# A smooth convolution of images 1 to 3 as 36 products of 256 columns instead of 24 of 512

## The chip, the cores and the metric

The kernel runs on one core of a Trainium2 chip. The core has five engines with an instruction queue each, worked through in order: TensorE (PE, matrix products into the eight PSUM banks), VectorE (DVE), ScalarE (ACT), GpSimd (POOL) and SyncE (SP), whose queue here only starts transfers. Queues wait for one another through semaphores. The metric is the device time of one execution, in microseconds.

## The reference, cut to what matters

Four images of 256 channels and 64 x 64 pixels go through four layers, each of which adds its result to its normalised input. Only the first layer's convolution is concerned here:

```python
xs = conv(group_norm(x), smooth_w, 3x3, SAME) + smooth_b
xs = relu(group_norm(xs, gn1_w, gn1_b))
theta, phi, g = conv1x1(xs) three times
attn = softmax(theta^T phi)                # 4096 x 4096 for each image
y = attn g;  x = x + 0.1 * group_norm(conv1x1(y)) + xs
```

Layer 1 is a linear attention, layer 2 a depthwise 3x3 convolution with generated taps and a generated pointwise product, layer 3 a mixture of four 1x1 convolutions. All is fp32.

## The kernel before, in words

**Stages.** Image 0 is convolved alone (`convolve_first`). Then, for each image b, `project` makes theta, phi and g in `tpg`, and `attend(b)` computes the softmax attention in 128 steps. A step makes four PE products: two `pf` (logits, L655), which ACT turns into exponentials `pr` (L656), and two `py` (L694); DVE adds `pr` to the running total `tot` (L118). After 16 steps a chunk of 512 columns ends (`ended`): `inv` on DVE (L663) closes the total, PE sums it over partitions (`pss`, L667), DVE takes the reciprocal (L669) and makes `yt`, PE makes `ps_wy` (L678). Each of these is one step behind the one before.

**Weaving.** Other work is woven between the steps of the attention. In round 0 that is `scale_weights` and the convolution of image 1; in rounds 1 and 2 the layers 1 to 3 of the image before (`tail`) and then the convolution of the next image; in round 3 a tail alone. The last tail has nothing beside it. A `Chain` sets the pace: woven code yields numbers, and `yield n` lets `n * rate` attention steps pass. `w.later(k, f)` runs f after k further steps. So the source order fixes every queue, and a larger rate spreads the woven work over more steps. The rates are 1.5, 0.86, 0.86 and 1.24. Woven work that is not through when a round's 128 steps are over goes on alone.

**Convolution by products.** It is in a Winograd form. Over rows it makes four output rows from six (`TY`, `MY` = 6, 4): `down(a)` forms six row combinations of the input on DVE, in `ra` and `rt`. Over columns it makes two output columns from four (`TX`, `MX` = 4, 2): `across(k)` forms the tile `v` by one DVE operation of 1024 elements. `products(a, k)` multiplies v by the transformed filter, for two output and two input halves of the channels, 512 columns each (L403); `joined` adds the PSUM banks into the output row a, and `joining(a)` combines the rows a into the four rows of the image. For image 0, `filter_down` and `filter_across` form the filters on DVE, and `filter_across` writes all of them to DRAM (`filters`); images 1 to 3 read them back, 128 KB at a time.

**Depthwise taps.** In `tail`, `taps` runs 64 operations of a row part each on DVE (`yield 0.62` after each), eight for each of eight parts; after every second part `pointwise` follows on PE one and two steps later (`ps_pw`, L979), and `pointwise_added` on DVE.

**Buffers.** `k4` is a pool of ten tiles of 1024 elements (pr, tot, v, dw and others), `k2` of six of 512, `u` of four filter tiles.

Of the kernel before, what the change touches and what calls it, by code (L numbers as in the profile page):

```python
# [8 lines left out]
F32 = mybir.dt.float32  # L9
# [25 lines left out]
TY, MY, TX, MX = 6, 4, 4, 2  # L35
IY, IX = HW // MY, HW // MX

# [53 lines left out]
def conv_preact_fast(ctx: ExitStack, tc: tile.TileContext, guard, x, wc, wtpg, ww, wqkv, wout, w1cat, wd2,  # L91
# [11 lines left out]
    def k4(name):  # L103
        return wk.tile([P, CH], F32, tag="k4", name=name, bufs=10)
# [3 lines left out]
    def k2(name):  # L108
        return wk.tile([P, 512], F32, tag="k2", name=name, bufs=6)
# [20 lines left out]
    ra = cp.tile([P, NH, IY, HW + 2], F32, name="ra")  # L130
# [105 lines left out]
    filters = tc.dram_tile([TY, NH, P, TX, NH, P], F32, name="filters")  # L236
# [30 lines left out]
    def filter_across(a, stay=False):  # L267

        ends = u1[:, a].rearrange("p h (j o) -> p h j o", j=3)
        s, mid = (t.rearrange("p (h o) -> p h o", h=NH)  # L270
                  for t in (wk.tile([P, 512], F32, tag="inv", name="ends2"), k2("middle") if a == 4 else junk()))
        if stay:
            both = [k2("both_u").rearrange("p (h o) -> p h o", h=NH) for _ in range(2)]
        else:
            t = k4("both_u").rearrange("p (b h o) -> p b h o", b=2, h=NH)
            both = [t[:, b] for b in range(2)]
        nc.scalar.mul(mid, ends[:, :, 1], 0.5)
        tt(s, ends[:, :, 0], ends[:, :, 2], ALU.add)
        stt(both[0], s, 0.5, mid, ALU.mult, ALU.add)
        stt(both[1], s, 0.5, mid, ALU.mult, ALU.subtract)  # L280

        def of(k):
            return both[k - 1] if k in (1, 2) else ends[:, :, 0 if k == 0 else 2]

        for oh in range(NH):
            for k in range(TX):
                nc.sync.dma_start(out=filters[a, oh, :, k], in_=of(k)[:, :, bass.ts(oh, P)])
        return lambda k, oh, h: of(k)[:, h, bass.ts(oh, P)]

# [84 lines left out]
    def across(k, rows):  # L374

        def col(j):
            return rows[:, :, :, j:j + MX * (IX - 1) + 1:MX]

        v = k4("v")
        first, second, op = ((0, 2, ALU.subtract), (1, 2, ALU.add), (2, 1, ALU.subtract), (1, 3, ALU.subtract))[k]  # L380
        tt(v.rearrange("p (h y x) -> p h y x", h=NH, x=IX), col(first), col(second), op)
        return v

    ACROSS = (1, 2, 0, 3)

    def joiner(st):

        dst, one = [None] * NH, [None] * NH
# [9 lines left out]
        def products(a, k, v, u):  # L398

            ps = [bank("ps_conv") for _ in range(NH)]  # L400
            for oh in range(NH):
                for h in range(NH):
                    nc.tensor.matmul(ps[oh], u(oh, h), v[:, bass.ts(h, 512)], start=(h == 0), stop=(h == NH - 1))  # L403
                if k == 1:
                    one[oh] = k2("one").rearrange("p (y x) -> p y x", x=IX)
                    nc.scalar.copy(one[oh], ps[oh].rearrange("p (y x) -> p y x", x=IX))
            return ps

        def joined(a, k, ps):

            for oh in range(NH):
                p = ps[oh].rearrange("p (y x) -> p y x", x=IX)
                if k == 2:
                    take(a, oh)
                even, odd = dst[oh][:, :, 0::2], dst[oh][:, :, 1::2]
                if k == 2:
                    tt(even, one[oh], p, ALU.add)
                    tt(odd, one[oh], p, ALU.subtract)
                elif k == 0:
                    tt(even, even, p, ALU.add)  # L420
                else:
                    tt(odd, odd, p, ALU.subtract)
            return list(dst)
# [19 lines left out]
        def joining(a, oh, t):  # L443

            y0, y1, y2, y3 = (image[:, oh, :, j, :] for j in range(MY))
            if a == 2:
                return [(tt, y2, y1, t, ALU.add), (tt, y1, y1, t, ALU.subtract), (tt, y0, y0, y2, ALU.add)]
            if a == 4:
                both = k4("both").rearrange("p (y x) -> p y x", x=HW)
                return [(tt, both, y3, t, ALU.add), (tt, y3, y3, t, ALU.subtract), (tt, y0, y0, both, ALU.add),  # L450
                        (stt, y2, both, 4.0, y2, ALU.mult, ALU.add), (stt, y1, y3, 2.0, y1, ALU.mult, ALU.add),
                        (stt, y3, y3, 6.0, y1, ALU.mult, ALU.add)]
            return [(tt, y3, y3, t, ALU.add)] if a == 5 else []
# [5 lines left out]
        return products, joined, row_products, rows_joined, joining, stats  # L459
# [36 lines left out]
    def convolve(w, b):  # L496
# [4 lines left out]
        products, joined, _, rows_joined, joining, stats = joiner(st)  # L501
        PRODUCTS = [(a, k) for a in range(TY) for k in ACROSS]

# [7 lines left out]
        def multiply(a, k, v, u):  # L511
            ps = products(a, k, v, u)
            if k != 1:
                w.later(1, lambda: join(a, k, ps))

        def join(a, k, ps):
            dst = joined(a, k, ps)
            if k == 3 and a == 4:
# [7 lines left out]
            elif k == 3 and a == 2:  # L526
# [4 lines left out]
            elif k == 3:  # L531
# [4 lines left out]
        def load_filters(i):  # L536
            res = []
            for oh in range(NH):
                u = wk.tile([P, NH, P], F32, tag="u", name="u", bufs=4)
                nc.sync.dma_start(out=u, in_=filters[PRODUCTS[i][0], oh, :, PRODUCTS[i][1]])  # L540
                res.append(u)
            return lambda oh, h: res[oh][:, h, :]
# [3 lines left out]
        for i, (a, k) in enumerate(PRODUCTS):  # L546
            if k == 1:
                for op, *args in down(a, ra, ra):
                    op(*args)
                    yield 0.35  # L550
            v, u = across(k, ra), us
            if i + 1 < len(PRODUCTS):
                us = load_filters(i + 1)
            w.later(1, lambda a=a, k=k, v=v, u=u: multiply(a, k, v, u))
            yield 0.8
# [4 lines left out]
    def convolve_first(w):  # L560
# [5 lines left out]
        def across_all(a, rows):  # L566
            return [(a, k, across(k, rows), lambda oh, h, k=k: u[a](k, oh, h)) for k in ACROSS]
# [5 lines left out]
        products, joined, row_products, rows_joined, _, stats = joiner(st)  # L573
# [5 lines left out]
        u = {a: filter_across(a, stay=True) for a in (4, 3)}  # L579
# [13 lines left out]
        for i, (a, k, v, f) in enumerate(four):  # L593
            if i + 1 < TX:
                joined(*three[i + 1])
            filter_across((0, 1, 2, 5)[i])
# [3 lines left out]
        for i in range(1, TX):  # L600
# [149 lines left out]
    def linear_attention(w, b, big, qT, k4, st, sh, alone):  # L750
# [25 lines left out]
        def qkv(xg, s2, rinv):  # L776
# [4 lines left out]
            for j in range(4):  # L781
# [8 lines left out]
                yield 0.125  # L790
# [22 lines left out]
        for c in range(NC):  # L813
            if c + 1 < NC:
                ahead = normed(c + 1)
            yield 0.5
# [244 lines left out]
    def mixed(w, b, big, k4, st, sh, held):  # L1061
# [39 lines left out]
        for h in range(NH):  # L1101
            wm.append(mix[:, h, :] if held is None else wk.tile([P, NH * P], F32, tag="u", name="wmh", bufs=4))
# [51 lines left out]

    def run(*steps):
# [16 lines left out]
    with tc.manual_schedule(engines={E.PE, E.Activation, E.DVE, E.Pool, E.SP}):  # L1172
        run(Chain(convolve_first).steps())
        run(project())
        for b in range(B - 1):
            attention = attend(b)
            parts = [tail(b - 1, big, qT)] if b > 0 else [scale_weights]
            if b == 0:
                load_x(1)
            run(Chain(both(*parts, lambda w: convolve(w, b + 1)), 1.5 if b == 0 else 0.86).steps(), attention)  # L1180
# [8 lines left out]
        run(Chain(tail(B - 2, big, qT, held=held), 1.24).steps(), attention)  # L1189
# [596 lines left out]
```

## Time and profile before

| what | us |
|---|---|
| median of 3 runs (lowest, highest) | 3144.46 (3142.55, 3146.85) |
| profiled execution (its span) | 3145.76 (3144.0) |
| PE, DVE, ACT busy in the span | 3033.0, 2079.6, 1129.2 |
| image 0 | 0 to 146 |
| round 0: image 1 beside attention of image 0 | 190.8 to 738 |
| round 1: tail of 0 and image 2 | 782 to 1479 |
| round 2: tail of 1 and image 3 | 1523 to 2219.9 |
| round 3: tail of 2 | 2263 to 2836 |
| end: tail of 3 alone | 2836 to 3144 |

Between these lie the four projects of some 44 us each. In the profile a product of two matrices counts as two PE instructions. A line of the groups names line, engine, operation, output and inputs with their sizes; then count, busy time, mean length in ns, and the idle time of the engine before such instructions with what ended it. In a line of busy times by stage stand its start and end, its length, the busy time and count of each engine, the granted PE clock, the share of the DMA engines and GB/s. In a line of the order of time stand start, length, engine and what ran.

### The profile page before, as it was taken

What the parts mean: (1) busy time and instruction counts of PE and PEld (TensorE: products, weight loads), DVE (VectorE), ACT (ScalarE), POOL (GpSimd) and SP (SyncE); (2) the same over time, 40 slices, a digit from 0 to 9 for tenths busy, and PEclk for the clock granted to TensorE, in tenths of its full rate; (3) what the DMA queues carried; (4) which work ended last, traced back from release to release, by engine and by line L of the source; (5) the groups of instructions that cost most, each with busy time, mean ns of one, the idle gap of its engine ahead of it and who ended that gap; (6) DMA issues with size and microseconds to landing.
All of it is one profiled execution on the core that took longest, in us unless ns stands there. A gap on an engine that the chain in (4) does not pass through costs nothing.

```text
span 3144.0 us, 24213 instructions
## 1 busy us (share of the span) xinstructions
PE 3033.0 (96%) x8526; PEld 1472.9 (47%) x8526; DVE 2079.6 (66%) x2611; ACT 1129.2 (36%) x2097; POOL 131.6 (4%) x175
## 2 busy tenths in 40 slices
PE   6899999999999999999999999999999999996888
PEld 3454444445564444444565444444545544443533
DVE  8736766443547995877536896778363768855485
ACT  2233224332555332323364432222445443333510
POOL 0000000000010000000011000000100100000100
PEclk9999999999999999999999999999999999998999
DMA  5610013001100023113300102310410010120011
GB/s 184 182 34 26 32 35 66 7 14 47 67 11 21 20 74 116 39 39 67 114 8 3 41 20 77 110 44 31 113 62 1 11 34 14 47 74 34 14 60 65
DMA packets 73985, 161.68 MB, mean 51 GB/s; under 512 B 7936, under 2 KB 39424, under 8 KB 70912
## 3 DMA queue, kind: packets, MB, share of 16 engines
q1 hardware_dynamic: 69248, 143.27, 13.3%
q0 software_dynamic: 4608, 16.78, 2.9%
q8 instruction: 70, 1.15, 0.2%
q14 instruction: 59, 0.48, 0.0%
HBM read 103.40 MB, written 73.40 MB: 56 GB/s over the span
## 4 chain that ended last, share of the span: by engine, by line
PE 80%; DVE 12%; issue 5%; ACT 2%; DMA 0%; POOL 0%; SPq 0%; POOLq 0%; ACTq 0%
PE pf L655 23%; PE py L694 23%; PE ps_conv L403 8%; PE ps_qkv L784 5%; DVE dw L121 4%; PE ps_tp L631 4%; PE ps_ex L1117 3%; PE ps_pw L979 3%; DVE tot L118 2%; PE ps_g L636 2%; PE ps_wy L678 2%; PE ps_o L852 1%; PE ps_ctx L806 1%; PE ps_dw L1014 1%; PE ps_ss L770 1%
## 5 line engine op out<-in xcount | busy, mean ns | idle before, releaser
L656 ACT ACTIVATE pr<-pf 128x512 f32<-128x512 f32 x1024 | 604.2, 596 | 1227.3 <-PE pf L655 1214.2
L655 PE MATMUL pf<-tpg 128*128 128x512 f32 x2048 | 967.2, 595 | 1.4 <-ACT pr L656 1.4
L694 PE MATMUL py<-pr,tpg 128*128 128x512 f32 x2048 | 962.1, 592 | 3.0 <-ACT pr L656 2.9
L118 DVE TENSOR_TENSOR tot<-tot,pr 128x1024 f32<-128x1024 f32 x448 | 546.3, 1219 | 249.7 <-ACT pr L656 248.1
L694 PEld LDWEIGHTS py<-pr,tpg 128*128 128x128 f32 x2048 | 388.8, 190 | 494.3 <-issue 479.8
L655 PEld LDWEIGHTS pf<-tpg 128*128 128x128 f32 x2048 | 381.5, 190 | 443.0 <-issue 419.1
L121 DVE SCALAR_TENSOR_TENSOR dw<-xp,dk,dw 128x1008 f32<-128x1008 f32 x216 | 272.9, 1267 | 6.8 <-ACT dw L971 3.7
L403 PE MATMUL ps_conv<-v,u 128*128 128x512 f32 x576 | 259.0, 596 | 3.6 <-DVE v L118 3.6
L403 PEld LDWEIGHTS ps_conv<-v,u 128*128 128x128 f32 x576 | 109.7, 191 | 143.5 <-issue 136.6
L784 PE MATMUL ps_qkv<-wqkv_s,xg 128*128 128x384 f32 x384 | 129.9, 487 | 0.0
L631 PE MATMUL ps_tp<-big,wtpg_s 128*128 128x512 f32 x256 | 118.0, 605 | 3.0 <-ACT big L492 3.0
L118 DVE TENSOR_TENSOR tpg<-ps_g,bg_s 128x512 f32<-128x512 f32 x32 | 22.1, 691 | 145.6 <-PE ps_g L636 145.6
L210 POOL TENSOR_TENSOR rstd<-rstd,half 128x2 f32<-128x2 f32 x24 | 16.8, 700 | 2419.3 <-DVE rstd L315 2225.7
L979 PE MATMUL ps_pw<-dw,pk 128*128 128x512 f32 x224 | 104.6, 601 | 8.1 <-DVE dw L121 8.1
L669 DVE RECIPROCAL inv<-pss 128x512 f32<-128x512 f32 x32 | 107.3, 3352 | 7.2 <-PE pss L667 7.2
L784 PEld LDWEIGHTS ps_qkv<-wqkv_s,xg 128*128 128x128 f32 x384 | 72.2, 190 | 53.6 <-issue 9.6
L794 DVE TENSOR_REDUCE qs<-qk 128x16 f32<-128x512 f32 x24 | 16.5, 686 | 119.0 <-ACT qk L788 119.0
L118 DVE TENSOR_TENSOR v<-ra 128x1024 f32<-128x1024 f32 x72 | 86.7, 1219 | 0.4
L632 ACT ACTIVATE tpg<-ps_tp,btp_s 128x512 f32<-128x512 f32 x64 | 43.9, 687 | 119.6 <-PE ps_tp L631 119.6
L631 PEld LDWEIGHTS ps_tp<-big,wtpg_s 128*128 128x128 f32 x256 | 47.9, 195 | 55.0 <-issue 50.6
L854 ACT ACTIVATE junk<-ps_o 128x256 f32<-128x256 f32 x128 | 49.2, 384 | 67.5 <-PE ps_o L852 59.4
L979 PEld LDWEIGHTS ps_pw<-dw,pk 128*128 128x128 f32 x224 | 43.0, 192 | 62.6 <-issue 51.9
(281 smaller groups left out, 2904.6 us busy)
## 6 DMA issues: line engine op xcount, KB each, us to landing
u<-filters SPq DMA_DIRECT2D x144, 128.0 KB, 2.3
xp<-in_x_dram SPq DMA_DIRECT2D x16, 1024.0 KB, 6.3
xs_d<-big POOLq DMA_DIRECT2D x32, 512.0 KB, 11.7
wy_d<-wt SPq DMA_DIRECT2D x32, 512.0 KB, 3.0
out_dram<-res SPq DMA_DIRECT2D x64, 256.0 KB, 2.0
wy<-wy_d SPq DMA_DIRECT2D x28, 512.0 KB, 5.2
xs<-xs_d SPq DMA_DIRECT2D x24, 512.0 KB, 5.3
wp<-in_wp_dram SPq DMA_DIRECT2D x16, 512.0 KB, 4.6
```

Source lines behind the costliest of these rows:

```text
L118: nc.vector.tensor_tensor(o, a, b, op)
L121: nc.vector.scalar_tensor_tensor(o, a, s, b, op0, op1)
L403: nc.tensor.matmul(ps[oh], u(oh, h), v[:, bass.ts(h, 512)], start=(h == 0), stop=(h == NH - 1))
L631: nc.tensor.matmul(ps, wtpg_s[:, h, k, :], big[:, h, cols], start=(h == 0), stop=(h == NH - 1))
L636: nc.tensor.matmul(ps[:, j, :], big[:, h, bass.ts(4 * c + j, P)], wtpg_s[:, h, 2, :], start=(h == 0), stop=(h == NH - 1))
L655: nc.tensor.matmul(pf, phi[:, bass.ts(2 * m + s, P)], theta[:, bass.ts(q, 512)], start=True, stop=True)
L656: nc.scalar.activation(pr[:, bass.ts(s, 512)], pf, AF.Exp)
L669: nc.vector.reciprocal(inv, pss)
L694: nc.tensor.matmul(py, g[:, bass.ts(2 * m + s, P)], probs[i][:, bass.ts(s, 512)], start=(m == 0 and s == 0), stop=(m == NM - 1 and s == 1))
L784: nc.tensor.matmul(ps[:, 0:3 * HID], xg[:, h, bass.ts(j, P)], wqkv_s[:, h, :], start=(h == 0), stop=(h == NH - 1))
L979: nc.tensor.matmul(ps, pk[:, h * NH * P + oh * P:h * NH * P + (oh + 1) * P], dw[h][:, bass.ts(s, 512)], start=(h == 0), stop=(h == NH - 1))
L1117: nc.tensor.matmul(ps, wm[h][:, bass.ts(oh, P)], big[:, h, cols], start=(h == 0), stop=(h == NH - 1))
```

## The change

For images 1 to 3 the column form becomes the one that the rows have: four output columns from six (`TX`, `MX` = 6, 4). There are then 36 products of 256 columns (6 rows x 6 columns), each again for two output and two input halves. Image 0 keeps the old form, under new names (`across_first`, `products_first`, `joined_first`, `ACROSS1`).

- `across(pair)` forms two columns k of v together, (1, 2), (3, 4) or (0, 5), by three or four DVE operations; its inputs are columns of `ra` at a step of four elements. `products` puts both output halves of one k in one PSUM bank. `joined` first makes the sum and difference of a pair in `sums` (ACT one part, DVE two), and after pair (3, 4) writes four output columns by four operations at a step of four elements (`put`); pair (0, 5) is added by two more. Rows 4 and 5 are collected in `rt` instead of k4 tiles.
- `filter_across` serves rows 4 and 3 of image 0 alone, and writes nothing. `keep` stores the six rows of `filter_down` in DRAM (`rows_d`, 768 KB each). `filters_across`, a new part of round 0 behind `scale_weights`, loads each row into `big`, makes the four inner columns by six DVE operations of 512 elements, and stores them (`filters`, 1 MB a row). The outer columns are read from `rows_d` itself. A filter load is now 256 KB.
- `k4` has nine buffers instead of ten, `k2` five instead of six; `u` keeps four, of twice the size.
- Rates: 1.36 in round 0; 0.66 for the tail and 0.79 for the convolution in rounds 1 and 2; 1.28 in round 3. In `linear_attention` two yields shrink, 0.125 to 0.08 and 0.5 to 0.25.

```diff
-TY, MY, TX, MX = 6, 4, 4, 2
+TY, MY, TX, MX = 6, 4, 6, 4
...
-        return wk.tile([P, CH], F32, tag="k4", name=name, bufs=10)
+        return wk.tile([P, CH], F32, tag="k4", name=name, bufs=9)
...
-        return wk.tile([P, 512], F32, tag="k2", name=name, bufs=6)
+        return wk.tile([P, 512], F32, tag="k2", name=name, bufs=5)
...
+    def keep(rows):
+        for a in rows:
+            nc.sync.dma_start(out=rows_d[a], in_=u1[:, a].rearrange("p h (j o) -> p h j o", j=3))
...
-        for oh in range(NH):
-            for k in range(TX):
-                nc.sync.dma_start(out=filters[a, oh, :, k], in_=of(k)[:, :, bass.ts(oh, P)])
...
+    def filters_across(w):
+        n = NH * 3 * NH * P
+        for a in range(TY):
+            t = big[:, a % 2, 0:n].rearrange("p (h j o) -> p h j o", h=NH, j=3)
+            f = big[:, a % 2, n:n + (TX - 2) * NH * NH * P].rearrange("p (k h o) -> p k h o", k=TX - 2, h=NH)
+            nc.sync.dma_start(out=t, in_=rows_d[a])
+            first, mid, last = (t[:, :, j, :] for j in range(3))
+            for op, *args in ((tt, f[:, 0], first, last, ALU.add), (tt, f[:, 1], f[:, 0], mid, ALU.subtract),
+                              (tt, f[:, 0], f[:, 0], mid, ALU.add), (stt, f[:, 2], last, 4.0, first, ALU.mult, ALU.add),
+                              (stt, f[:, 3], mid, -2.0, f[:, 2], ALU.mult, ALU.add),
+                              (stt, f[:, 2], mid, 2.0, f[:, 2], ALU.mult, ALU.add)):
+                op(*args)
+                yield 0.3
+            nc.sync.dma_start(out=filters[a], in_=f)
...
+    def across(pair):
+        v = k4("v").rearrange("p (k n) -> p k n", k=2)
+        def cols(j):
+            return ra.rearrange("p h y x -> p (h y) x")[:, :, j:j + HW].rearrange("p r (i k) -> p k r i", k=MX)[:, 0:2]
+        vt = v.rearrange("p k (r i) -> p k r i", i=IX)
+        one, two = v[:, 0], v[:, 1]
+        def each(j, f, other):
+            return [(stt, vt[:, i], cols(j)[:, i], f, other[:, i], mul, add) for i in range(2)]
+        ops = {0: lambda: each(2, -5.0, cols(4)) + each(0, 4.0, vt),
+               1: lambda: each(1, -4.0, cols(3)) + [(tt, one, one, two, add), (stt, two, two, 2.0, one, mul, sub)],
+               3: lambda: [(tt, vt, cols(3), cols(1), sub), (stt, one, one, 2.0, two, mul, add),
+                           (stt, two, two, 2.0, one, mul, sub)]}
+        return v, ops[pair[0]]()
...
+        def products(pair, v, u):
+            banks = []
+            for i in range(2):
+                ps = bank("ps_conv")
+                for oh in range(NH):
+                    for h in range(NH):
+                        nc.tensor.matmul(ps[:, bass.ts(oh, IY * IX)], u[i][:, h, bass.ts(oh, P)],
+                                         v[:, i, bass.ts(h, IY * IX)], start=(h == 0), stop=(h == NH - 1))
+                banks.append(ps)
+            if pair != (0, 5):
+                parts[pair] = k4("sums").rearrange("p (k n) -> p k n", k=2)
+                nc.scalar.mul(parts[pair][:, 0], banks[0], -1 / 6 if pair == (1, 2) else 1 / 24)
+            return banks
...
+                    o = to[:, :, j::MX]
+                    stt(o, t, f, o if other is None else other, ALU.mult, ALU.add)
+            if pair == (0, 5):
+                put((0, 0.25, ps[0], None), (3, 1.0, ps[1], None))
+            elif not end:
+                stt(s[:, 1], ps[1], -f, s[:, 0], ALU.mult, ALU.add)
+                stt(s[:, 0], ps[1], f, s[:, 0], ALU.mult, ALU.add)
+            else:
+                near, far = parts[1, 2], parts[3, 4]
+                put(*((j, f, far[:, j % 2], near[:, j % 2]) for j, f in enumerate((1.0, 2.0, 4.0, 8.0))))
...
-            v, u = across(k, ra), us
+            (v, ops), u = across(pair), us
             if i + 1 < len(PRODUCTS):
                 us = load_filters(i + 1)
-            w.later(1, lambda a=a, k=k, v=v, u=u: multiply(a, k, v, u))
-            yield 0.8
+            for op, *args in ops:
+                op(*args)
+                yield 0.4
+            w.later(1, lambda a=a, pair=pair, v=v, u=u: multiply(a, pair, v, u))
+            yield 1
...
-                yield 0.125
+                yield 0.08
...
-            yield 0.5
+            yield 0.25
...
-            parts = [tail(b - 1, big, qT)] if b > 0 else [scale_weights]
+            parts = [at(0.66, tail(b - 1, big, qT))] if b > 0 else [at(1.36, both(scale_weights, filters_across))]
...
-            run(Chain(both(*parts, lambda w: convolve(w, b + 1)), 1.5 if b == 0 else 0.86).steps(), attention)
+            parts.append(at(1.36 if b == 0 else 0.79, lambda w: convolve(w, b + 1)))
+            run(Chain(both(*parts)).steps(), attention)
...
-        run(Chain(tail(B - 2, big, qT, held=held), 1.24).steps(), attention)
+        run(Chain(tail(B - 2, big, qT, held=held), 1.28).steps(), attention)
```

## The prediction

> **What bounds the kernel now.** I read the page's busy line and its chain first, then busy time by stage, then the order of time on PE and DVE inside a stage.
>
> ```profile
> PE 3033.0 (96%) x8526; PEld 1472.9 (47%) x8526; DVE 2079.6 (66%) x2611; ACT 1129.2 (36%) x2097; POOL 131.6 (4%) x175
> ...
> PE 80%; DVE 12%; issue 5%; ACT 2%; DMA 0%; POOL 0%; SPq 0%; POOLq 0%; ACTq 0%
> ...
> L403 PE MATMUL ps_conv<-v,u 128*128 128x512 f32 x576 | 259.0, 596 | 3.6 <-DVE v L118 3.6
> ```
>
> PE carries the chain, and the products to be changed are 259 us of it. By stage (image 0; project; rounds 0 to 3 with the projects between them; the end):
>
> ```profile
> core 0: us, PE busy (x) PEld busy (x) DVE busy (x) ACT busy (x) POOL busy (x), PEclk, DMA share, GB/s
> 0.00:146.00 146.00, 113.89 (x264) 50.82 (x264) 123.77 (x166) 26.90 (x39) 3.42 (x21) 0.98 0.54 186
> ...
> 190.80:738.00 547.20, 543.65 (x1272) 240.82 (x1271) 323.98 (x344) 185.35 (x310) 8.36 (x10) 1.00 0.10 26
> ...
> 782.00:1479.00 697.00, 689.49 (x1897) 329.62 (x1897) 515.77 (x646) 264.39 (x493) 33.08 (x39) 1.00 0.15 48
> ...
> 1523.00:2219.90 696.90, 689.40 (x1895) 329.40 (x1895) 515.89 (x647) 264.39 (x493) 33.10 (x39) 1.00 0.15 48
> ...
> 2263.00:2836.00 573.00, 573.00 (x1630) 279.77 (x1630) 371.47 (x456) 244.17 (x469) 27.18 (x29) 1.00 0.10 35
> ```
>
> In rounds 0 to 2, where the change works, PE idles 3.6 + 7.5 + 7.5 us. So a microsecond taken from PE is gained only while DVE keeps pace. Round 1 cut into 20.5 us pieces shows how near that is:
>
> ```profile
> 1069.00:1089.50 20.50, 20.50 (x49) 9.11 (x48) 20.29 (x21) 8.17 (x14) 0.00 (x0) 1.00 0.00 0
> 1089.50:1110.00 20.50, 20.50 (x49) 9.12 (x48) 20.22 (x21) 5.71 (x10) 0.00 (x0) 1.00 0.00 0
> ...
> 1438.00:1458.50 20.50, 19.18 (x47) 8.45 (x46) 20.33 (x31) 5.97 (x10) 0.00 (x0) 1.00 0.00 0
> ```
>
> The first two lie in the depthwise taps of the tail: both engines are full. The third is the end of the convolution: DVE is full and PE has begun to lose (1.3 us). The order of time gives the prices:
>
> ```profile
> 930.80 1.89 PE L852 MATMUL ps_o<-w,xp 128*128 128x256 f32 x8
> 932.53 1.88 PE L655 MATMUL pf<-tpg 128*128 128x512 f32 x4
> 934.25 1.88 PE L694 MATMUL py<-pr,tpg 128*128 128x512 f32 x4
> ```
>
> ```profile
> 1088.24 1.22 DVE L118 TENSOR_TENSOR tot<-tot,pr 128x1024 f32<-128x1024 f32 x1
> 1089.38 2.58 DVE L121 SCALAR_TENSOR_TENSOR dw<-xp,dk,dw 128x1024 f32<-128x1024 f32 x2
> 1091.88 1.22 DVE L118 TENSOR_TENSOR tot<-tot,pr 128x1024 f32<-128x1024 f32 x1
> ```
>
> Eight 256-column instructions start 1.73 us before the next group, so 0.216 us each; four of 512 take 1.72 us, 0.43 each (each product is two instructions). Half the columns cost half, weight load included. One attention step is 3.43 us of PE. On DVE, one tot and two taps take 3.64 us; back to back, an instruction starts some 0.04 us before its predecessor's recorded end.
>
> [...] the trace's 512-element rows have 683 to 692, so cutting an operation in two costs an extra 0.16 us. [...] The new column operations step by four fp32[...]. The trace has stride two at full speed (v<-ra, 1219 ns, like the contiguous tot) and no stride four. [...] 128 KB land in 2.3 us, 512 KB in 4.6 to 5.2, 1024 KB in 6.3.
>
> **The change, part by part.**
>
> *Products.* Per image 96 x 2 instructions of 512 (192 x 0.43 = 82.4 us) become 144 x 2 of 256 (288 x 0.216 = 62.3). Saved: 20 us an image, **60 us** in rounds 0 to 2, if PE does not wait instead.
>
> *DVE work of a convolution.* Removed per image: 24 x 1.22 (v) + 48 x 0.683 (joins out of PSUM) = 62 us. Added: 6 x 1.22 + 60 x 0.69 (v) + 60 x 0.69 (sums and results) = 90 us. The row-joining operations keep their number, and ACT swaps 12 copies for 12 scalings (0.59 each). So +28 us of DVE an image against -20 of PE. Mean load hides that; what stretches cannot hide follows.
>
> *Rates, rounds 1 and 2.* The order of DVE's instructions against the attention steps shows the tail ending near step 62 instead of 86, and products at steps 75 to 120 instead of 96 to 117. A tap (0.62 of a yield) now takes 0.62 x 0.66 = 0.41 steps, before 0.53. Taps stretch now: 64 taps and 8 pk sums fill 28 steps. PE: 28 x 3.43 + 64 x 0.43 (pointwise) + two chunk ends of 2.6 = 129 us. DVE: 64 x 1.265 + 8 x 0.75 + 16 x 1.37 (pointwise joins and statistics) + 26 tots x 1.22 + two chunk ends x 6.1 (reciprocal 3.35 and the rest) = 153, less 156 x 0.04 = 147. The excess is 18 us. Before, with 36.5 steps, PE had 158 and DVE 157: the full-but-free picture above. Each pointwise product stands one step behind its last tap and PE is in order, so behind a late tap wait pointwise, then pf and py. Lag is not carried over: **18 us** of waiting a round.
>
> The convolution keeps its mean: now 49 steps with PE 239 and DVE 219, before 24 steps with 168 and 154, 92% each. But the lumps grow. The row-4 joining beside a chunk end and the next rows has 65 us of DVE in ten steps with 51 of PE; the row-2 joining with a chunk end 24 in three steps with 11. In the old kernel such excesses of up to about 6 us passed with 1.3 us lost. I take 14 - 6 and 13 - 6, **15 us**, less the 2.5 lost now.
> Rounds 1 and 2 together: 2 x (-20 + 18 + 15 - 2.5) = **+21 us**.
>
> *Filters of image 1 formed in round 0.* Six rows, each: load 768 KB, six DVE operations of 512 (4.1 us), store 1 MB. On SP the load of a row stands behind the store of the row before, which waits for that row's last operation; behind the row's first operation on DVE stand the tots and the chunk's end (inv, reciprocal, yt), and for those PE waits at pss and ps_wy. No such transfer is in the trace; from 512 and 1024 KB I take 6 us with the store beside it (bounds 4 and 8), 0.7 for two issues. A row thus needs 6.7 + 4.1 + 2.45 tots x 1.14 - 0.6 run in the wait = 13 us, while its 2.45 steps (six yields of 0.3 at rate 1.36) are 8.4 us of PE. The first row's load is early (big is free when the project ends); it ends 21 us into the round. Four rows on, inv is done at 72 us; PE reaches pss after 17 steps, at 58: 14 us. The sixth load then lies ahead of the reciprocal: 8 more at ps_wy. **+22 us** (10 to 34). Row-4 lump of this round: +5. Round 0: -20 + 22 + 5 = **+7 us**.
>
> *Image 0.* 12 operations of 0.69 us and 48 stores leave DVE and SP; six stores come. PE runs there without a gap from 25 to 137 us, so nothing; without that cover a gain of at most 8 us.
>
> *Pools, round 3, end.* One buffer fewer in k4 and k2, and linear attention in half the steps. Round 3's PE is at 573 of 573 and qkv itself fills PE. I take 0; bounds 0 and +10.
>
> Sum: 21 + 7 = +28, taken as +24, because lag can partly pass through the pr buffers between two product waits. The profiled execution is 3145.8 us (span 3144.0), the median of the runs 3144.5: **3168 us**.
>
> **The rivals.**
> *Stride four is slow (25%).* Per image 24 576 elements of v and 18 432 of results lie on stride four; [...] the same stretch sums add some 14 us to each of rounds 1 and 2 and 4 to round 0: 3200, at half that price 3184. [...] Against: no run shows it, and writes may differ from reads.
> *DVE's lag is carried (25%), faster.* The place is the pr buffers: if PE may run several steps ahead past the pointwise and pss waits, lumps vanish and the rates' excess is half absorbed: 9 a round, with loads of 4 us (10 in round 0): -60 + 10 + 18 = 3112. It decides where all returned waits stay under 60 us. For: 140 us of full DVE cost PE about nothing before. Against: there DVE and PE were equal, not 147 to 129.
> *The two cancel (8%).* Waits of 54 to 66 us: 3138 to 3151.
> That 256 columns do not cost half is excluded by the ps_o group.
>
> **How the numbers follow.** Forecast 42% (its own range 3151 to 3186), stride 25%, carried lag 25%, cancelling 8%. Below the range of 3108 to 3215 lies the carried lag with every load hidden, above it a full stride price on both sides with the k4 bound; each about one in ten. A measurement tells some 0.2% (6 us) from no change. Faster 25%, same 8%, slower 67%.
>
> **What would show it.** Right: products at about 62 us an image; PE idle up from 7.5 to some 35 us in rounds 1 and 2, ended by dw at the pointwise products, by v, yt and inv; in round 0 DVE idle before the filter sums, ended by the load of rows, and PE idle at pss and ps_wy. The new 512-element operations at 0.69 us deny the stride rival, 0.95 to 1.2 prove it. Wrong: rounds 1 and 2 shorter than 741 us with PE still full while DVE runs at 100%, or filter loads landing before they are asked for.

## The result, and the profile after

The changed kernel takes 3236.9 us (median of 4 runs, 3234.2 to 3239.2) against 3145.4 (3142.6 to 3146.9): the ratio is 1.029 [1.027, 1.031]. It is slower by some 91 us, where 24 were forecast, and lies above the range of 3108 to 3215. The profiled executions are 3237.4 and 3144.0 us long, 93.4 apart.

The page of the kernel after has these lines for busy time, the chain and two groups of products:

```profile
PE 3026.9 (93%) x8814; PEld 1548.4 (48%) x8814; DVE 2262.7 (70%) x2797; ACT 1128.2 (35%) x2093; POOL 124.6 (4%) x175
...
PE 67%; DVE 24%; issue 5%; ACT 2%; DMA 1%; POOL 0%; SPq 0%; POOLq 0%; DVEq 0%; ACTq 0%
...
L447 PE MATMUL ps_conv<-v,u 128*128 128x256 f32 x864 | 205.6, 392 | 17.6 <-DVE v L126 6.5
...
L1070 PE MATMUL ps_pw<-dw,pk 128*128 128x512 f32 x224 | 112.9, 638 | 24.4 <-DVE dw L126 24.4
```

The products of the convolution have shrunk from 259.0 us to 205.6, yet PE is busy for only 6 us less, and DVE's part of the chain has doubled (12% before). The pointwise products wait 24.4 us for taps (8.1 before). The stages, in the same form as before:

```profile
core 0: us, PE busy (x) PEld busy (x) DVE busy (x) ACT busy (x) POOL busy (x), PEclk, DMA share, GB/s
...
191.30:744.00 552.70, 529.78 (x1366) 262.24 (x1365) 400.20 (x434) 185.66 (x310) 8.37 (x10) 0.98 0.19 58
...
788.50:1526.50 738.00, 692.09 (x1986) 355.99 (x1986) 572.36 (x700) 264.86 (x493) 30.37 (x39) 0.97 0.16 50
...
2352.00:2930.00 578.00, 574.66 (x1622) 279.98 (x1621) 371.90 (x456) 243.84 (x467) 25.54 (x29) 0.99 0.11 35
```

Rounds 1 and 2 take 738 us each: +41 and +41.1, where +10.5 each was forecast. Round 0 is +5.5 (forecast +7), round 3 +5 (forecast 0), everything else together +0.8. So the miss lies mainly in rounds 1 and 2, which take 61 us more than forecast. In round 1 PE idles 738.0 - 692.1 = 45.9 us (7.5 before), and it is busy 2.6 us longer than before although 20 us of products are gone. The waits of PE in round 1 (engine and tile, what was late, then us, times, longest):

```profile
PE pm L325 <- DVE mv L123: 13.2, 4, 4.3
PE ps_pw L1070 <- DVE dw L126: 8.1, 2, 4.9
PE pss L758 <- DVE inv L754: 4.4, 2, 2.6
PE py L785 <- ACT pr L747: 4.0, 3, 1.8
PE ps_zt L966 <- DVE z L123: 3.3, 3, 3.0
PE ps_conv L447 <- DVE v L126: 3.3, 2, 2.3
PE ps_conv L447 <- issue: 3.0, 1, 3.0
```

Three kinds and a rest add up to 45.9. `ps_pw`, `pss` and `ps_wy` (2.6) wait 15.1 us, all but 0.6 of it in the stretch of taps. The convolution's products wait 7.1 (for 3.0 of it the profile names no releaser; the last operation on their `v` had ended 0.1 us before). And small products that stand right behind a statistic or a small matrix (`pm`, `ps_zt`, `pv` and four lesser ones) wait 19.7; in the kernel before those were 4.9. They belong to the tail, but for one `pm` of 3.5 us at the end of the convolution. The last 4.0 are `py`. Why PE is busy longer stands in the order of time behind one of these waits (start, length, instruction, and the idle time ahead of it in brackets):

```profile
819.05 1.88 PE L785 MATMUL py<-pr,tpg 128*128 128x512 f32 x4
825.19 0.59 PE L325 MATMUL pm<-mv,avg 128*128 128x2 f32 x2 [4.27 <-DVE mv L123]
826.99 0.59 PE L334 MATMUL pv<-ev,avg 128*128 128x2 f32 x2 [1.21 <-DVE ev L123]
827.44 3.76 PE L746 MATMUL pf<-tpg 128*128 128x512 f32 x4
830.99 3.02 PE L785 MATMUL py<-pr,tpg 128*128 128x512 f32 x4
```

The same four products take 1.88 us before the pause, and 3.76 and 3.02 after it. The granted clock was 0.50 from 827.4 to 831.0 us and 0.62 from 831.0 to 834.0: 3.0 us are lost on top of the wait. Over round 1 this is 2.6 + 20.4 = 23 us (20.4 is what the products save where nothing waits, shown below); a granted clock of 0.97 over 738 us says the same, 22. So -20.4 for products, +38.4 for idle time and +23 for the clock make the +41.

What makes the wait of 4.27 us at `pm` stands in the busy times of the stretch ahead of it, in which DVE forms the layer's input and its statistics. The first line is the kernel before, the second the kernel after:

```profile
792.00:820.90 28.90, 28.90 (x69) 12.57 (x67) 28.84 (x36) 10.15 (x17) 0.00 (x0) 1.00 0.54 182
...
797.90:825.10 27.20, 22.42 (x52) 9.42 (x50) 27.00 (x34) 7.09 (x13) 0.00 (x0) 0.96 0.56 193
```

Before, both engines are full, and `pm` follows without a wait. After, DVE is as full, but at the lower rate the stretch holds only 22.4 us of PE. So here too DVE has more to do than PE, in a stretch that the forecast did not sum.

In round 0 the filter loop waits as forecast. What the sums of filters (`big`) on DVE waited for, and then PE at the first chunk's end:

```profile
  DMA big<-rows_d: 31.6, 5
```

```profile
265.89 2.07 PE L758 MATMUL pss<-inv,ones 128*128 128x512 f32 x2 [13.85 <-DVE inv L754]
267.76 3.04 PE L746 MATMUL pf<-tpg 128*128 128x512 f32 x4
...
281.23 3.78 PE L769 MATMUL ps_wy<-yt,ww_s 128*128 128x512 f32 x4 [5.29 <-DVE yt L123]
```

The waits were forecast as 14 and 8. Here too the groups behind them run slow: `pf` takes 3.04 us and `ps_wy` 3.78, where four such products take 1.88 at a granted clock of 1.00. The clock was 0.75 from 266 to 274 us and 0.66 from 281.2 to 290. Last, the stride. Two groups of the page, the first without a step, the second reading at a step of four:

```profile
L126 DVE SCALAR_TENSOR_TENSOR sums<-ps_conv,sums 128x512 f32<-128x512 f32 x72 | 49.7, 691 | 61.7 <-PE ps_conv L447 55.3
...
L126 DVE SCALAR_TENSOR_TENSOR v<-ra 128x512 f32<-128x512 f32 x72 | 76.2, 1089 | 0.1
```

The rival of the slow stride was right that the step costs time: 1089 ns against 691, inside its 0.95 to 1.2.

### The profile page after: what moved, and what is told of

Read it like the earlier page. It is cut to its first block, busy times and chain, and to the rows that moved or that the text cites. A ratio compares the mean times of both kernels' runs of the same rounds, so it can differ in the third digit from the quotient of the medians.

```text
span 3237.4 us, 24824 instructions
## 1 busy us (share of the span) xinstructions
PE 3026.9 (93%) x8814; PEld 1548.4 (48%) x8814; DVE 2262.7 (70%) x2797; ACT 1128.2 (35%) x2093; POOL 124.6 (4%) x175
## 4 chain that ended last, share of the span: by engine, by line
PE 67%; DVE 24%; issue 5%; ACT 2%; DMA 1%; POOL 0%; SPq 0%; POOLq 0%; DVEq 0%; ACTq 0%
PE pf L746 19%; PE py L785 19%; PE ps_qkv L875 5%; DVE dw L126 5%; PE ps_conv L447 5%; DVE tot L123 4%; PE ps_tp L722 3%; PE ps_ex L1208 3%; DVE big L126 2%; PE ps_pw L1070 2%; PE ps_g L727 2%; DVE big L123 2%; DVE inv L760 1%; PE ps_wy L769 1%; DMA big<-rows_d 1%
## 5 line engine op out<-in xcount | busy, mean ns | idle before, releaser
L746 PE MATMUL pf<-tpg 128*128 128x512 f32 x2048 | 987.3, 605 | 0.5 <-DVE z L123 0.4
L746 PEld LDWEIGHTS pf<-tpg 128*128 128x128 f32 x2048 | 391.3, 194 | 439.1 <-issue 412.7
L447 PE MATMUL ps_conv<-v,u 128*128 128x256 f32 x864 | 205.6, 392 | 17.6 <-DVE v L126 6.5
L447 PEld LDWEIGHTS ps_conv<-v,u 128*128 128x128 f32 x864 | 168.6, 196 | 68.1 <-issue 29.4
L1070 PE MATMUL ps_pw<-dw,pk 128*128 128x512 f32 x224 | 112.9, 638 | 24.4 <-DVE dw L126 24.4
L126 DVE SCALAR_TENSOR_TENSOR sums<-ps_conv,sums 128x512 f32<-128x512 f32 x72 | 49.7, 691 | 61.7 <-PE ps_conv L447 55.3
L769 PE MATMUL ps_wy<-yt,ww_s 128*128 128x512 f32 x128 | 64.8, 631 | 14.5 <-DVE yt L123 14.5
L126 DVE SCALAR_TENSOR_TENSOR v<-ra 128x512 f32<-128x512 f32 x72 | 76.2, 1089 | 0.1
```

Of the source, the lines that this page charges most:

```text
L126: nc.vector.scalar_tensor_tensor(o, a, s, b, op0, op1)
L447: nc.tensor.matmul(ps[:, bass.ts(oh, IY * IX)], u[i][:, h, bass.ts(oh, P)], v[:, i, bass.ts(h, IY * IX)], start=(h == 0), stop=(h == NH - 1))
L746: nc.tensor.matmul(pf, phi[:, bass.ts(2 * m + s, P)], theta[:, bass.ts(q, 512)], start=True, stop=True)
L769: nc.tensor.matmul(ps, ww_s[:, bass.ts(h, P)], yt, start=True, stop=True)
L1070: nc.tensor.matmul(ps, pk[:, h * NH * P + oh * P:h * NH * P + (oh + 1) * P], dw[h][:, bass.ts(s, 512)], start=(h == 0), stop=(h == NH - 1))
```

## The experiments

The first three experiments set two theories against each other. By A the slow stride makes most of the loss. By B the tail's new pace does, since PE waits in rounds 1 and 2 where DVE has more to do, with the stride and the filter loop as smaller parts. Later ones ask which side of the pace it is: the sum of DVE's work in a stretch, or the distance of products behind their inputs. Each ratio is to the kernel before.

### The stride alone

Columns lie side by side instead of four apart. The kernel leaves out the right places of the columns, so its output is another; number and size of all instructions are as in the kernel after.

```diff
-            return ra.rearrange("p h y x -> p (h y) x")[:, :, j:j + HW].rearrange("p r (i k) -> p k r i", k=MX)[:, 0:2]
+            return ra.rearrange("p h y x -> p (h y) x")[:, :, j:j + 2 * IX].rearrange("p r (k i) -> p k r i", k=2)
...
-                    o = to[:, :, j::MX]
+                    o = to[:, :, bass.ts(j, IX)]
```

> The changed kernel, but the column reads of the convolution and its column results run over 32 or 16 neighbouring elements instead of a step of four; the result is another, every instruction, count and wait is the same. Theory A (stride): operations at a step of four cost 1.09 us instead of 0.69, some 100 us of DVE in three images, and this makes most of the loss: the time falls to 3150 to 3175, and the waits of PE in the second half of rounds 1 and 2 vanish. Theory B (order: the tail's new rates and the filter loads make most of it): only those waits go, 17 us in rounds 1 and 2 and 5 in round 0: 3190 to 3205.

3210.5 us, ratio to before 1.021 [1.020, 1.023]: the stride costs 26 us, less than either theory said and nearer to B. The operation, and round 1 between its projects, in the kernel after and here:

```profile
L126 DVE SCALAR_TENSOR_TENSOR v<-ra 128x512 f32<-128x512 f32 x72 | 47.2, 684 | 0.1
...
786.80:1526.50 739.70, 693.79 (x2002) 357.60 (x2001) 572.36 (x700) 265.55 (x494) 30.37 (x39) 0.97 0.16 50
...
782.30:1510.90 728.60, 687.32 (x2002) 355.14 (x2002) 542.04 (x700) 265.44 (x494) 30.37 (x39) 0.98 0.16 50
```

The same operation takes 684 ns, 0.40 us less. In round 1 DVE is busy 30 us less (542.0 for 572.4), but the round is only 11 us shorter (728.6 for 739.7). So the stride is a part, and the smaller one.

### The filter row loaded ahead

```diff
+        def load(a):
+            t = big[:, a % 2, 0:n].rearrange("p (h j o) -> p h j o", h=NH, j=3)
+            nc.sync.dma_start(out=t, in_=rows_d[a])
+            return t
...
+        ahead = load(0)
         for a in range(TY):
-            t = big[:, a % 2, 0:n].rearrange("p (h j o) -> p h j o", h=NH, j=3)
+            t = ahead
+            if a + 1 < TY:
+                ahead = load(a + 1)
...
-            nc.sync.dma_start(out=t, in_=rows_d[a])
```

> The changed kernel with each filter row's load put ahead of the sums of the row before on SP's queue; nothing else. Theory B (the load behind the store sets the wait): PE's waits at pss and ps_wy in round 0 (19 us) and the slow PE clock after them (some 5 us) go: 3237 falls to about 3213. Rival (the transfers themselves or the six operations a row are too slow): under 8 us gained, 3229 or more.

3210.3, ratio 1.021 [1.019, 1.023]: 27 us back, about what was expected. Round 0, cut from the end of one project to the start of the next:

```profile
189.60:718.70 529.10, 525.31 (x1384) 261.60 (x1383) 400.81 (x434) 186.30 (x311) 8.36 (x10) 1.00 0.19 59
```

By the same cut round 0 is 549.3 before and 554.8 after. With the load issued a row early PE idles 3.8 us, hardly more than the 3.6 before, and what is left is the gain of the products in full: 20.2 us of time, 20.4 of PE's busy time. The loop's cost was thus 25.7 us in this round: 19.1 of waits and 6.6 of slow PE work behind them (PE busy for 531.9 us in the kernel after at a granted clock of 0.98, for 525.3 here at 1.00).

### The tail's pace alone

The kernel before, with its old convolution, in the new pace of the tail. The convolution runs at rate 1.5 in rounds 1 and 2, so that it ends where it did.

```diff
-                yield 0.125
+                yield 0.08
...
-            yield 0.5
+            yield 0.25
...
-            parts = [tail(b - 1, big, qT)] if b > 0 else [scale_weights]
+            parts = [at(0.66, tail(b - 1, big, qT))] if b > 0 else [at(1.5, scale_weights)]
...
-            run(Chain(both(*parts, lambda w: convolve(w, b + 1)), 1.5 if b == 0 else 0.86).steps(), attention)
+            parts.append(at(1.5 if b == 0 else 1.5, lambda w: convolve(w, b + 1)))
+            run(Chain(both(*parts)).steps(), attention)
...
-        run(Chain(tail(B - 2, big, qT, held=held), 1.24).steps(), attention)
+        run(Chain(tail(B - 2, big, qT, held=held), 1.28).steps(), attention)
```

> The kernel before with only the tail's new pace: 0.66 in rounds 1 and 2, the two shorter yields, 1.28 in round 3, and 1.5 for the convolution there so that it still ends near step 121. Theory B: the pace alone costs 20 to 25 us in each of rounds 1 and 2: 3185 to 3195, with PE waiting for dw at the pointwise products. Theory A (the tail's pace is harmless, the stride makes the loss): within 6 us of 3145.

3237.9, ratio 1.030 [1.028, 1.031]. The pace alone, without any of the new arithmetic, costs as much as the whole change: right in direction, twice the size expected. In the kernel after, then, the gain of the products and the costs of the new arithmetic and of the filter loop nearly cancel; that is a difference of totals, as stretches overlap. Round 1 between its projects, in the kernel before and here:

```profile
781.10:1479.20 698.10, 690.59 (x1906) 330.55 (x1906) 515.95 (x647) 265.08 (x494) 33.08 (x39) 1.00 0.15 48
...
782.00:1526.80 744.80, 708.67 (x1908) 337.59 (x1907) 519.77 (x647) 265.30 (x494) 30.37 (x39) 0.97 0.15 46
```

Of the 47 us 29 are waits and 18 lowered clock (the same products keep PE busy for 708.7 us instead of 690.6).

### Which part of the pace

Four kernels take the pace apart. First, the two old yields of the linear attention are put back, all rates as squeezed:

```diff
-                yield 0.08
+                yield 0.125
...
-            yield 0.25
+            yield 0.5
```

> The squeezed tail with the two old yields of the linear attention (0.125 and 0.5) again, the rates as squeezed. If the rate of 0.66 makes the loss: 3215 to 3235, hardly below the 3238 of the squeezed tail. If the shortened yields make it (all 64 products of q, k and v within 3 steps): 3150 to 3185.

3241.5, ratio 1.031 [1.029, 1.033]: the yields are not it, the rate is. But a rate does two things: it puts more of DVE's work into a step, and it shortens the distance between a statistic and the product that needs it. So the second kernel keeps the squeezed taps and doubles the distances:

```diff
-        yield 1
+        yield 2
...
-                    w.later(1 + s, lambda c=c, s=s, d=d: pointwise(c, s, d))
+                    w.later(2 + s, lambda c=c, s=s, d=d: pointwise(c, s, d))
...
-            parts.append(at(1.5 if b == 0 else 1.5, lambda w: convolve(w, b + 1)))
+            parts.append(at(1.5 if b == 0 else 0.86, lambda w: convolve(w, b + 1)))
```

(The first edit is made at thirteen `yield 1`, most of them between a statistic or small matrix and its product. As the tail then takes more steps, round 3 runs at 1.05.)

> The kernel before with the squeezed tail (taps at rate 0.66, convolution at its old 0.86), but every product that waits for a statistic or a small matrix stands two yields behind it instead of one, and each pointwise product one step further behind its last tap. Theory 'sum' (the stretch of taps has 18 us more of DVE than of PE, wherever the products stand): rounds 1 and 2 still lose 18 us of waits and some 8 us of lowered clock each, 720 to 728, total 3190 to 3205. Theory 'distance' (products stand so close behind their inputs that each waits 2 to 4 us and is followed by slow PE work): rounds 1 and 2 back at 697 to 706, total 3144 to 3162.

3172.2, ratio 1.009 [1.007, 1.010]: between the two theories, nearer to "distance". Some 66 of the 93 us are back, with every tap and rate of the tail kept. Round 1 is 713.2. Its main waits:

```profile
PE ps_wy L678 <- DVE yt L118: 8.5, 1, 8.5
PE pss L667 <- DVE inv L663: 5.2, 1, 5.2
PE pm L304 <- DVE mv L118: 1.8, 1, 1.8
```

`pm` fell from 10.5 to 1.8 and the pointwise waits are gone; the lag of the taps (13.7 us, where the forecast had 18) now ends at the next chunk's end in two large pauses. As the convolution's pace was changed too, the third kernel changes only that, and spaces nothing:

```diff
-            parts.append(at(1.5 if b == 0 else 1.5, lambda w: convolve(w, b + 1)))
+            parts.append(at(1.5 if b == 0 else 0.86, lambda w: convolve(w, b + 1)))
```

> The squeezed tail with the convolution at its old pace (0.86 instead of 1.5), nothing spaced. In the spaced kernel both were changed. The squeezed tail's round 1 shows 4.4 us of waits in the convolution and perhaps 3 of clock behind them. If the spacing of the products won back the time there: 3220 to 3238. If the convolution's pace did: 3165 to 3185.

3240.2, ratio 1.030 [1.028, 1.032]: nothing. The spacing did it. It both moves a product further behind its input and gives the tail more steps, so that PE has more to do in a stretch such as the one ahead of `pm`; the runs do not part these two. The fourth takes only the other half away, the crowded taps:

```diff
-                yield 0.62
+                yield 0.8
```

(with 1.35 for the convolution and 1.1 in round 3)

> The squeezed tail with only the taps at about their old pace (a yield of 0.8 instead of 0.62 at rate 0.66; convolution 1.35, round 3 at 1.1), nothing spaced. The waits in the stretch of taps are 13.8 us in round 1 of the squeezed tail. If the sum of DVE in the taps is an independent part: 13.8 and some 8 of clock go in each of two rounds, and 5 in round 3: 3185 to 3200. If the taps' own sum doesn't matter and the close products of the rest make the loss: 3220 to 3238.

3206.6, ratio 1.019 [1.018, 1.021]: 31 us back, less than the 38 or more expected. Round 1 gains 12 us; the waits for `pm` stay at 10.8, and those of `ps_wy` rise from 3.7 to 7.0. So of the squeezed tail's 47 us in round 1 relief for the taps is worth 12 and the spacing 32. Both are there, and the spacing, which the forecast did not have, is the larger.

### What a pause costs beyond itself

Seven small products are added to round 3 of the kernel before, each behind a DVE copy and a reciprocal.

```diff
+            if b == B - 1 and i % 16 == 8 and 8 < i:
+                wait = k2("pause")
+                nc.vector.tensor_copy(wait, probs[i][:, 0:512])
+                for _ in range(1):
+                    nc.vector.reciprocal(wait, wait)
+                pz = bank("ps_pause")
+                nc.tensor.matmul(pz[:, 0:2], ones, wait[:, 0:2], start=True, stop=True)
```

> The kernel before with seven extra small products in round 3, each waiting for a DVE copy and one reciprocal of 512 elements (0.7 + 3.4 us) of the step before it; round 3 has PE at 573 of 573 without it. PE idles about 2 us at each, 14 in all. [...] 3144 + 14 = 3158, no slow work behind. If a pause of 2 us is enough: 12 to 20 us more, 3170 to 3178, and the groups behind a pause take 2.6 to 3.8 us instead of 1.88.

3165.7, ratio 1.006 [1.005, 1.008], between the two. The order of time shows why (three of the seven):

```profile
2397.20 0.35 PE L706 MATMUL ps_pause<-pause,ones 128*128 128x2 f32 x2 [3.24 <-DVE pause L704]
2397.42 5.81 PE L791 MATMUL ps_qkv<-wqkv_s,xg 128*128 128x384 f32 x12
...
2495.46 0.38 PE L706 MATMUL ps_pause<-pause,ones 128*128 128x2 f32 x2 [2.98 <-DVE pause L704]
2495.70 1.07 PE L882 MATMUL ps_zt<-ident,z 128*128 128x128 f32 x8
...
2573.64 0.58 PE L706 MATMUL ps_pause<-pause,ones 128*128 128x2 f32 x2 [6.29 <-DVE pause L704]
2574.09 3.76 PE L655 MATMUL pf<-tpg 128*128 128x512 f32 x4
2577.64 2.93 PE L694 MATMUL py<-pr,tpg 128*128 128x512 f32 x4
```

Twelve `ps_qkv` products take 4.03 us earlier in this round, where the granted clock is 1.00; here 5.81, 1.8 more, with a clock of 0.91 from 2390 to 2410 us. After 6.29 us of pause the next two groups lose 1.88 + 1.05. The pause of 2.98 us and four shorter ones (0 to 0.9) are followed by nothing. In these pauses the length would part the two kinds. Three others don't fit that, the first in round 0 of the kernel before (granted clock 0.68 from 389.8 to 395.2 us), the second in round 1 of the kernel after with its granted clock, the third in the last kernel of the next section:

```profile
389.83 5.40 PE L403 MATMUL ps_conv<-v,u 128*128 128x512 f32 x8 [1.90 <-DVE v L118]
...
1460.52 3.03 PE L447 MATMUL ps_conv<-v,u 128*128 128x256 f32 x8 [2.32 <-DVE v L126]
1463.35 2.58 PE L746 MATMUL pf<-tpg 128*128 128x512 f32 x4
...
1461.30:1464.70 3.40, 3.40 (x8) 2.25 (x7) 3.37 (x5) 0.00 (x0) 0.00 (x0) 0.50 0.00 0
...
1452.47 0.38 PE L333 MATMUL pm<-mv,avg 128*128 128x2 f32 x2 [3.67 <-DVE mv L123]
1452.71 1.96 PE L754 MATMUL pf<-tpg 128*128 128x512 f32 x4
```

After 1.90 us eight products take 5.40 instead of 3.60 us, after 2.32 us two groups lose 1.14 + 0.70, and after 3.67 us none is lost. So a pause of 1.90 us was enough in one place, and one of 3.67 us passed in another. The length of a pause does not settle it alone, and what does stays open. Where the clock fell behind these pauses, 1.8 to 2.9 us were lost.

### The new form at other paces

First the kernel after with the old pace of the tail, and the convolution in the 26 steps that this leaves:

```diff
-            parts = [at(0.66, tail(b - 1, big, qT))] if b > 0 else [at(1.36, both(scale_weights, filters_across))]
+            parts = [at(0.86, tail(b - 1, big, qT))] if b > 0 else [at(1.36, both(scale_weights, filters_across))]
...
-            parts.append(at(1.36 if b == 0 else 0.79, lambda w: convolve(w, b + 1)))
+            parts.append(at(1.36 if b == 0 else 0.46, lambda w: convolve(w, b + 1)))
```

(with the old yields, and 1.24 in round 3)

> The kernel after with the old pace of the tail (0.86, old yields) and the convolution in the 26 steps that are left (rate 0.46; 1.24 in round 3). If only the tail's pace costs time: rounds 1 and 2 at 700 to 712 each, total 3160 to 3185. If the convolution's own sum of DVE decides (26 steps: DVE about 159 + 14 for stride four + 32 of tots + two chunk ends of 6, some 215, against PE 62 + 89 + 5 = 156): waits of 45 to 60 us and a lowered clock in each of rounds 1 and 2, 735 to 755 each, total 3230 to 3270.

3234.5, ratio 1.028 [1.027, 1.030]: as the sum of DVE said. Three pieces of its convolution:

```profile
1300.00:1320.00 20.00, 17.38 (x45) 9.41 (x44) 19.83 (x20) 4.63 (x8) 0.00 (x0) 0.91 0.09 27
...
1360.00:1380.00 20.00, 14.07 (x41) 7.60 (x40) 19.90 (x20) 3.58 (x6) 0.00 (x0) 0.96 0.08 26
...
1440.00:1460.00 20.00, 15.38 (x48) 9.70 (x48) 19.79 (x21) 3.59 (x6) 0.00 (x0) 0.91 0.09 27
```

DVE is full, PE is at 14 to 17 of 20 us, and the clock falls as well. The loss has moved from the tail into the convolution. Round 3 has its old pace here, but the smaller pools: from the last `ps_tp` to the last `py` it takes 577.2 us, as before (577.1). The squeezed tail with the old pools has 582.2. So the 5 us of round 3 are the pace, and the pools cost nothing.

Then a pace in between, with the loads ahead, the taps at about their old pace and more distance behind statistics and taps:

```diff
-        yield 1
+        yield 1.6
...
-                yield 0.62
+                yield 0.8
...
-                    w.later(1 + s, lambda c=c, s=s, d=d: pointwise(c, s, d))
+                    w.later(2 + s, lambda c=c, s=s, d=d: pointwise(c, s, d))
...
-            parts.append(at(1.36 if b == 0 else 0.79, lambda w: convolve(w, b + 1)))
+            parts.append(at(1.36 if b == 0 else 0.68, lambda w: convolve(w, b + 1)))
```

(the first edit is the one between `mv` and `pm`; round 3 at 1.1)

> The kernel after with loads ahead, the taps back at about their old pace (a yield of 0.8 at rate 0.66), statistics and pointwise products standing further behind their inputs, and the convolution in the 39 steps from 84 to 123. Theory 'sum by stretch': the taps and the small products lose nothing more, but the convolution has DVE 147 + 22 for the stride + 48 of tots + 12 of chunk ends = 229 us against PE 62 + 134 + 5 = 201: 28 us of waits and some 10 of lowered clock; rounds 1 and 2 at 690.6 - 20 + 7.5 + 38 = 716 each, total 3155 to 3165. Theory 'mean load' (572 us of DVE against 670 of PE in the round; only the placing of products costs time): 680 to 690 each, total 3085 to 3110.

3159.7, ratio 1.005 [1.003, 1.007]; round 1 takes 715.9, where 716 was worked out. The stretch ahead of the taps, the taps' and the convolution's:

```profile
759.00:1001.00 242.00, 228.33 (x800) 125.23 (x799) 145.15 (x228) 122.45 (x261) 21.28 (x28) 0.98 0.11 36
1001.00:1151.00 150.00, 149.31 (x351) 66.07 (x349) 139.14 (x144) 49.14 (x81) 0.39 (x1) 1.00 0.10 38
...
1241.00:1475.00 234.00, 218.73 (x629) 122.13 (x628) 223.43 (x242) 63.34 (x106) 1.87 (x3) 0.96 0.13 39
```

The taps lose nothing now. The convolution, with DVE at 95%, loses 15 us of waits and has the lowered clock (0.96 of 234 us, some 9 more): 24 where 38 were forecast. The stretch ahead of the taps still waits 13.7 us, where nothing more was to be lost than the 7.5 of the whole round before. So the sum came out, in part by luck, and its parts did not.

> The same with columns side by side instead of at a step of four elements, so that the outputs' columns are in other places: DVE 207 against PE 201 in the convolution. Sum by stretch: 22 us of DVE less in a stretch that DVE fills are nearly 22 us of time and some clock, in each of two rounds: 3100 to 3120. Mean load: the stride changes nothing, as mid.

With the columns side by side (the edit of the first experiment, and again an output with its columns elsewhere): 3136.9, ratio 0.998 [0.997, 0.999]. Of 30 us of DVE a round 12 came back as time (715.9 to 703.8), as in the first experiment, and not the 20 expected; the total lies between the two theories.

### The new form for image 1 only

Round 0 has DVE to spare (324 of 547 us before), rounds 1 and 2 have not. So image 1 takes the new form with loads ahead; images 2 and 3 keep the old form (`convolve_two`) and pace, the tail and round 3 their old yields and rates, and both sets of filters are stored; the smaller pools stay.

```diff
-            parts = [at(0.66, tail(b - 1, big, qT))] if b > 0 else [at(1.36, both(scale_weights, filters_across))]
+            parts = [at(0.86, tail(b - 1, big, qT))] if b > 0 else [at(1.36, both(scale_weights, filters_across))]
...
-            parts.append(at(1.36 if b == 0 else 0.79, lambda w: convolve(w, b + 1)))
+            parts.append(at(1.36, lambda w: convolve(w, 1)) if b == 0 else at(0.86, lambda w: convolve_two(w, b + 1)))
```

> The new form for image 1 alone, with the filter loads put ahead; images 2 and 3 and the tail's pace as before, filters of both forms stored; nine k4 and five k2 buffers. Theory: round 0 has room on DVE, so it gains the 20 us of products less some 5 at the lump of row 4, and rounds 1 and 2 stay: 3128 to 3133. Rival (the buffers or the second set of filters cost): 3145 or more.

3123.9, ratio 0.994 [0.992, 0.995]: faster than both kernels, and a little better than expected. Rounds 0 and 1:

```profile
189.80:718.90 529.10, 525.32 (x1384) 261.62 (x1383) 400.85 (x434) 186.25 (x311) 8.35 (x10) 1.00 0.19 59
761.60:1459.90 698.30, 690.67 (x1906) 330.55 (x1905) 516.17 (x647) 264.51 (x494) 33.16 (x39) 1.00 0.15 49
```

Round 0 gives its 20 us, round 1 is as it was.

## Why the prediction was wrong, step by step

**Products: right.** 20 us an image were forecast, 20.2 were measured where nothing waits.

**DVE work: half of it missing.** +28 us an image; in round 1 it is +56.6 (572.4 for 515.8). The stride is the other half (30); without it +26 are left. The slow stride was named as a rival with a chance of 25% and left out of the likeliest sum. Its price (14 a round, 4 in round 0, 32 in all) rested on an assumption of the author's about the step, which no trace of the kernel before shows; it was near the 11, 10 and 5 measured.

**Rates, rounds 1 and 2: here it failed.** The step had 18 for taps and 15 for lumps of the convolution, less 2.5, +10.5 a round after the products. Measured in round 1: taps 15.1, convolution 7.1. Both are the right mechanism, the second half the size. Two terms were left out, and no reason was given. Small products right behind their statistics wait 19.7 us, 4.9 before: the forecast summed DVE's work for the taps and for the convolution, but not for a stretch such as the one ahead of `pm` (27.0 us of DVE, 22.4 of PE), and it did not ask how short a lower rate makes the distance of a product behind its input. And PE runs slow behind many of the pauses (granted clock 0.97 over round 1, 0.50 in the two stretches read above): 23 us a round, the largest term of the miss, and a cost that no wait shows. In the kernel before with the squeezed tail, spacing the products gave back 32 of 47 us a round, which confirms the first term there; no run spaces the products of the kernel after and changes nothing else. The slow groups behind the pauses show the second.

**Filters formed in round 0: right.** +22 was forecast, in the places where it came (14 and 8 at `pss` and `ps_wy`; 13.9 and 5.3 measured); the cost of 25.7 includes 6.6 for the clock, which was not forecast. The row-4 lump of 5 is a single wait of 3.5 us at a product of the convolution in the kernel with image 1 alone, and two waits of 3.6 us that round 0 had before are gone there. So +7 came near the +5.5 partly because these two errors cancel.

**Image 0, pools: right.** Both are nothing. **Round 3** is +5 within its bounds, but for the pace and not for the pools.

**The sum.** +28 was taken as +24 because lag might pass through. It went the other way: slow PE work follows many waits (23 us in round 1). The "carried lag" rival is refuted where DVE has more to do than PE: in the kernel with spaced products the lag of the taps did pass the pointwise products, and came back whole at the next chunk's end (8.5 and 5.2 us).

What stays open: why 30 us of DVE a round bring only 11 to 12 us of time when the stride is taken away. That part of these operations run where DVE has room is likely, but no run here counts them. Open too is what, besides its length, decides whether a pause is followed by the lower clock.

## What to carry to other kernels

A pace for woven work sets two things, how much an engine has to do in a stretch and how far a product stands behind its input; work both out for every stretch, and look for the waits at small products as well as at the large ones. Behind pauses of 1.90, 2.32, 3.24, 4.27 and 6.29 us PE lost another 1.8 to 3.0 us here, behind others of 2.98 and 3.67 nothing, so price the clock behind a wait as well as the wait. When an exchange takes PE time for DVE time, make it where DVE has room: in round 0 it gained its 20 us, in rounds 1 and 2 no pace tried here gained anything.

## What the hardware showed that was not expected

- Operations of 512 elements at a step of four fp32 elements on DVE took 0.40 us longer than with the columns side by side (1089 for 684 ns), 0.79 ns an element, on the side read (v) as on the side written (results, 1098 for 684), and also where the other operand comes from PSUM (1086 for 686). A step of two had no price in the kernel before (`v`, 1219 ns for 1024, as `tot` without a step).
- PE ran slow behind single pauses of 1.90, 2.32, 3.24, 4.27 and 6.29 us, and not behind others of 2.98 and 3.67, in the middle of kernels whose PE is busy for 93 to 96% of the time. The granted clock was 0.68 behind the first, 0.50 behind the second and fourth, and 0.91 in the 20 us around the third; behind the last, four products took 3.76 us for 1.88. 1.8 to 3.0 us were lost each time. Over the kernel after, the mean granted clock was 0.969, for 0.987 before.
